# Both query halves of a head pair in one stage, for batches 0 and 1 as well

## The chip, the core and the metric

The kernel runs on one core of one Trainium2 chip. The metric is the device time of one execution in microseconds (us). The median of three runs of the kernel before is 2141.41 us (2141.41 to 2141.47). Everything is computed in fp32.

## What is computed

The inputs are x (16 batches of 1024 nodes with 256 channels), a sparse-valued 1024 x 1024 matrix adj that is stored dense, and small weights. There are two layers, each ended by a LayerNorm over the channels. Cut to what matters:

```python
# layer 0, for each batch; fea is x transposed (256 x 1024)
c_adj = mean(fea, axis=1)                      # one mean for each node
A  = |(|sigmoid(c_j - c_i) - 0.5|) - 0.5| * 2  # 1024 x 1024
g  = relu((fea @ (adj * sym(A))) * para)       # "query graph": q = g transposed
k, v = split(x @ kv_w)                         # 4 heads of 64 channels
out = softmax(q k^T * scale) v
x1  = layernorm(x + out)
# layer 1
h = relu(x1 @ w1_loop + adj @ (x1 @ w1_neigh) + b1)
h = relu(h  @ w2_loop + adj @ (h  @ w2_neigh) + b2)
y = layernorm(x1 + (x1 + h) * 0.5)
```

## The kernel before

**The order of work.** `run()` (L1029) writes the order of all instructions by hand: it stands under a manual schedule, so each engine works its own queue strictly in the order of the program text. The engines are TensorE (PE), VectorE (DVE), ScalarE (ACT), GpSimd (POOL), and SyncE (SP), which issues the DMAs. For each batch b there are five blocks of work: the attention of b, layer 1 (the graph convolution) of earlier batches, the query graph of b+1, the LayerNorm of b, and the keys and values of b+1.

**The attention** (class `Attention`, L623). The four heads form two head pairs, and the 1024 queries two halves of 512, so there are four units, numbered 2 * pair + half. `scores(u)` (L637) makes for each of eight key tiles two matmuls, one for each head of the pair; each uses 64 of the 128 rows of the array, so that two run side by side. ACT takes the exponential into an SBUF tile `pr`, and DVE adds the eight `pr` tiles up (`collect`, L665) and folds the sum into `den_part` (`partial`, L674). `outputs(u)` (L687) multiplies the `pr` tiles with v into one PSUM tile `av`, `turn(u)` (L700) transposes it on DVE into a tile `o`, and `add(units)` (L705) sums the denominators with one small matmul into `den_ps`, takes reciprocals, scales `o` and adds it to x (the tile `xB`). That last step is the "fold" of a unit. A batch can do a unit at a time (scores, outputs), or both halves of a pair: `both_scores(pair)` (L683) makes 16 score tiles in a row, and `two_units(pair)` (L1109) then makes both outputs. Before the change, batches 0 and 1 go a unit at a time, and batches 2 to 15 take both halves.

**PSUM** has eight banks of 512 fp32 values for each partition. The kernel cuts them into three "big" tiles of two banks (`big_psum`, `half_psum`, L85 to L89) and two "bank" tiles of one bank (`bank_psum`, L91). A score tile takes a big tile; but under `both_scores` every fourth one, from the third on, is *split* and takes the two bank tiles instead (L643 to L645). A tile can be taken again only when its last reader is through.

**SBUF rows.** Most working tiles (pr, adj, wg, o of even units, xB and so on) come from one pool of 31 row tiles (`row_tile`, L99).

**The query graph.** In batch 0 the class `Queries` (L483) builds the queries of batch 1: for each of eight row tiles t it loads a tile of adj, makes the likeness on ACT (two activations), multiplies by adj on DVE (`times_adj`, L513), and does four matmuls (`step`, L517), which accumulate into two big PSUM tiles `g_ps`; `end` (L526) reads them on DVE. Later batches use `FastQueries` (L533) with fewer multiplications.

**The LayerNorm of layer 0** (`BlockedNorm`, L319): `mean` and `squares`; `sum_squares` on DVE; `variance` (L343), which is a small matmul into `sum2`, one DVE instruction that writes `rstd`, and a power of -0.5 of a 128 x 32 tile on POOL (L347); `scale` (L349), two DVE multiplications by that result; and `spread` (L354), two DVE transposes and eight DMAs that store it.

**Keys and values of the next batch** (`KeysValues.run`, L428): seven products for each, in a Strassen-like form, with PSUM tiles `k_ps` (big) and `v_ps` (bank). It takes two callbacks, `between` after the fifth pair of products and `later` after the sixth. Four DVE additions stand behind `later` in the text, and the last two of them are the last readers of a big tile (`k_next`) and of a bank tile (`v_next`):

```python
            between()
            k_next, v_next = half_psum(f"k_ps_{b}_2"), bank_psum(f"v_ps_{b}_2")
...
            later()
            add(kT[:, 1, FB:N], u3, p7)
            add(block(1, 1), tiles(z3), tiles(y7))
...
            add(kT[:, 1, 0:FB], u1, k_next)
...
            add(block(1, 0), tiles(z1), tiles(v_next))
```

In batch 0 `later` holds `norm.scale()`, `norm.spread()` and four DVE transposes of adj tiles (`turn_adj((2, 3))`); `norm.variance()` is called earlier, ahead of `step(7)`. In batches 1 to 14 the order is `kv.run(norm.variance, q.scale)`, with `norm.scale` and `norm.spread` after `kv.run`.

**Layer 1** (`GraphConv`, L790): batch 1 does the first half of batch 0's convolution alone (`inner`, `first`); from batch 2 on `Joined` (L957) shares the products with adj between two batches. The last batch ends in `ending` (L910), which puts the bias b2 into PSUM by ACT (`bias`, L935) and lets the matmuls of `outer` (L870) accumulate onto it.

Of the kernel before, what the change touches and what calls it, by code (L numbers as in the profile page):

```python
# [10 lines left out]
F32 = mybir.dt.float32  # L11
# [7 lines left out]
def kernel(  # L19
# [603 lines left out]
    class Attention:  # L623
# [76 lines left out]
        def turn(self, u):  # L700
            name, pav = f"o_{self.b}_{u}", self.o[u]
            self.o[u] = work.tile([P, FB], F32, tag="o", name=name) if u % 2 else row_tile(name)[:, 0:FB]
            nc.vector.transpose(self.o[u], pav)
# [86 lines left out]
    class GraphConv:  # L790
# [68 lines left out]
        def second(self, quarters, between=None):  # L859

            self.uT = row_tile(f"uT_{self.b}")
            for j in range(NJ):
                pu = half_psum(f"u_ps_{self.b}_{j}")
                self.neighbours(j, pu, range(TJ), quarters)
                if j and between:
                    between()
                self.neighbours(j, pu, range(TJ, NT), quarters)
                nc.scalar.copy(self.uT[:, ts(j, FB)], pu)

        def outer(self, g, per, p2, onto=False):  # L870
            for i in range(per):
                t = g * per + i
                nc.tensor.matmul(p2[:, ts(i, C)], self.uT[:, ts(t, P)], w2n_sb, start=not onto, stop=False,
                                 skip_group_check=onto)
                nc.tensor.matmul(p2[:, ts(i, C)], self.h1T[:, ts(t, P)], w2l_sb, start=False, stop=True,  # L875
                                 skip_group_check=onto)
# [8 lines left out]
        def last(self):  # L885
            per = N // C
            for g in range(NT // per):
                p2 = big_psum(f"h2_ps_{self.b}_{g}")
                self.outer(g, per, p2)
                self.residual(g, per, p2)  # L890

# [18 lines left out]
        def ending(self, dst, quarters, aside):  # L910
# [24 lines left out]
            def bias(g):  # L935
                banks[g] = (bank_psum if g % 2 else half_psum)(f"h2e_ps_{g}")
# [14 lines left out]
            self.second(quarters, lambda: (bias(0), bias(1), aside(), bias(2), bias(3), quarter(0)))  # L951
# [77 lines left out]
    def run():  # L1029
# [57 lines left out]
        for b in range(B):  # L1087
# [30 lines left out]
            if more and not c1:  # L1118
                for u in range(len(UNITS)):
                    att.scores(u)  # L1120
                    if u:
                        att.add(u - 1)
                    att.outputs(u)
                    if u == 2:
                        for t in range(3):
                            q.load(t)
                            q.weigh(t)
                    if u == 0:
                        NodeSums(q, xb, str(b + 1)).all()
            elif more and not both:  # L1130
                att.scores(0)
                att.outputs(0)
                NodeSums(q, xb, str(b + 1)).all()
                kv = KeysValues(b + 1, channel_major(blocked, f"xT_{b + 1}"))
                att.scores(1)
                kv.sums()
                att.add(0)
                att.outputs(1)
                for t in (0, TJ):
                    q.load(t)  # L1140
                c1.inner()
                q.left(nc.gpsimd)
                for t in (0, TJ):
                    q.likeness(t)
                for ij, n in QUARTERS.items():
                    store(n, quarters[ij])
                c1.first(quarters, lambda: (att.add(1), adj_sums(quarters, 1), adj_sums(quarters, 2), weigh_first()))
                c1.turn_blocks()
                att.scores(2)
                att.outputs(2)  # L1150
                for t in (1, TJ + 1):
                    q.load(t)
                    q.likeness(t)
                    q.times_adj(t)
                att.scores(3)
                for t in (2, TJ + 2, 3, TJ + 3):
                    q.load(t)
                for t in (2, TJ + 2, 3, TJ + 3):
                    q.likeness(t)
                q.right(1)  # L1160
                att.add(2)
                att.outputs(3)
            elif more:
# [6 lines left out]
                both.fetch("00", "10")  # L1170
                c2.load_x()
# [7 lines left out]
                both.fetch(2, 3)  # L1179
                nodes.line()  # L1180
                both.fetch(1)
                nodes.row()
                for t in (0, TJ):
                    q.load(t)
                both.fetch(4, "11")
                c1.inner()
                both.left(nc.gpsimd)
                both.run({1: (lambda: q.left(nc.gpsimd),),
                          2: (lambda: att.add(0, 1),),
                          6: (lambda: q.likeness(0), lambda: c3 and c3.moments()),  # L1190
                          7: (lambda: q.likeness(TJ),),
                          5: (weigh_first,),
                          4: (lambda: c3 and c3.finish(out[b - 3]),)})
                c2.last()
# [20 lines left out]
            if more and not c1:  # L1215
# [8 lines left out]
                q.times_adj(4)  # L1224
                q.step(1)
                att.add(3)
# [4 lines left out]
                q.times_adj(5)  # L1231
                q.step(2)
                q.step(3)
                norm.mean()
                q.times_adj(6)
                q.times_adj(7)
                q.step(4)
                norm.squares()
                norm.sum_squares()
                q.step(5)  # L1240
# [3 lines left out]
                norm.variance()  # L1244
                xB = load_blocked(b + 1, f"a{b + 1}")
                q.step(7)
                qT = q.end()
                load_next()
                kT, v = kv.run(later=lambda: (norm.scale(), norm.spread(), turn_adj((2, 3))))
                turn_adj((5, 6, 7))  # L1250
            elif more:
                q.pair(2)
                q.step(0)
                q.step(1, lambda: att.add(*((2, 3) if both else (3,))), 5)
# [37 lines left out]
        c2.last()  # L1292
        c1.turn(1)
        c2.moments()
        c1.ending(out[B - 1], quarters, lambda: c2.finish_aside(out[B - 2]))
# [70 lines left out]
```

## Time and profile before

| What | Value |
|---|---|
| Median of the runs | 2141.41 us |
| The profiled execution: time, span of its instructions | 2141.32 us, 2139.5 us (1.8 us lie around the span) |
| Busy: PE, DVE, ACT, POOL | 2127.3, 1889.8, 1046.4, 342.9 us |
| Mean granted TensorE clock | 0.998 of full speed |
| Batch 0, attention (first score matmul to first `g_ps` matmul) | 49.70 to 107.05 us |
| Batch 0, query graph, and keys and values | 107.05 to 135.29, 135.29 to 147.73 us |
| Batch 1, attention with the convolution of batch 0 | 147.73 to 225.90 us |
| Batch 1, query graph, and keys and values | 225.90 to 250.49, 250.49 to 263.15 us |
| Batch 2 begins | 263.15 us |
| Last matmul of the convolution begins | 2128.33 us |

"Busy" of PE counts every matmul from its start to its modelled end, so 99% does not say that the array runs at its peak: a stage in which PE waits a little between matmuls shows up as a longer stage. It is read from the start times of one stage and the next. In the timeline a line is a run of equal instructions: start, time from the first to the last end, engine, source line, operation, output and inputs, shapes, count; the brackets give the idle time of the engine ahead of it and what ended it. A 512-column fp32 matmul is recorded as two instructions.

### The profile page before, as it was taken

The numbers are of one execution on the slowest core, as the hardware profiler recorded it, in microseconds if no ns is written. First come the engines' busy times: TensorE is split into PE (matmuls) and PEld (weight loads), VectorE is DVE, ScalarE is ACT, GpSimd is POOL, SyncE is SP. The second block draws the span as 40 slices with busy tenths as digits, with TensorE's granted clock in tenths as the row PEclk, the third lists the DMA queues.
The fourth block names the chain that finished last, engine by engine and source line by source line (L and its number), as shares of the span: only waits on it lengthen the run. The fifth ranks groups of instructions, "written<-read, shape, count | busy, mean of one in ns | idle before, by whom it ended". The sixth has DMA issues, their size and how long they took to land.

```text
span 2139.5 us, 24050 instructions
## 1 busy us (share of the span) xinstructions
PE 2127.3 (99%) x8356; PEld 1028.0 (48%) x8356; DVE 1889.8 (88%) x2360; ACT 1046.4 (49%) x1486; POOL 342.9 (16%) x187
## 2 busy tenths in 40 slices
PE   9999999999999999999999999999999999999998
PEld 5344444544445455454554444544445444544454
DVE  5999998989899898988989899899898999989964
ACT  5745545545355452555625555355553445545412
POOL 1011120121302113030130301303012130121021
PEclk9999999999999999999999999999999999999999
DMA  9495675737677365763747638466473665734544
GB/s 236 128 141 185 133 224 139 180 123 124 208 165 208 95 123 212 158 217 97 140 177 156 217 118 152 154 148 216 131 173 130 138 217 146 180 118 96 163 157 157
DMA packets 611393, 341.09 MB, mean 159 GB/s; under 512 B 491712, under 2 KB 556608, under 8 KB 611264
## 3 DMA queue, kind: packets, MB, share of 16 engines
q1 hardware_dynamic: 610992, 339.21, 60.5%
q8 instruction: 68, 1.11, 0.2%
q14 instruction: 61, 0.50, 0.1%
q10 hardware_dynamic: 272, 0.26, 0.0%
HBM read 289.54 MB, written 49.87 MB: 159 GB/s over the span
## 4 chain that ended last, share of the span: by engine, by line


## 5 line engine op out<-in xcount | busy, mean ns | idle before, releaser
L672 DVE TENSOR_TENSOR acc<-acc,pr 128x1024 f32<-128x1024 f32 x384 | 473.2, 1232 | 37.1 <-ACT pr L656 0.7
L658 ACT ACTIVATE pr<-s 128x1024 f32<-128x1024 f32 x400 | 397.4, 1116 | 143.7 <-PE s L651 143.7
L651 PE MATMUL s<-qT,kT 64*128 64x512 f32 x2048 | 450.3, 593 | 0.0
L693 PE MATMUL av<-pr,v 128*64 128x512 f32 x2048 | 447.4, 594 | 0.0
L651 PEld LDWEIGHTS s<-qT,kT 64*128 64x128 f32 x2048 | 196.1, 187 | 236.4 <-issue 182.2
L693 PEld LDWEIGHTS av<-pr,v 128*64 128x64 f32 x2048 | 143.8, 137 | 295.6 <-issue 271.6
L347 POOL TENSOR_TENSOR rstd<-rstd,neg_half 128x32 f32<-128x32 f32 x16 | 99.8, 6236 | 1118.7 <-DVE rstd L345 1118.7
L988 PE MATMUL hu_ps<-adj,R 128*128 128x512 f32 x480 | 211.8, 594 | 0.0
L509 ACT ACTIVATE wg<-c_row,c_sums 128x1024 f32<-128x1024 f32 x120 | 137.0, 1142 | 85.6 <-DVE den_part L680 65.8
L515 DVE SCALAR_TENSOR_TENSOR wg<-wg,adj 128x1024 f32<-128x1024 f32 x128 | 150.1, 1210 | 11.8 <-ACT wg L510 11.8
L988 PEld LDWEIGHTS hu_ps<-adj,R 128*128 128x128 f32 x480 | 90.1, 190 | 108.1 <-issue 105.0
L510 ACT ACTIVATE wg<-wg 128x1024 f32<-128x1024 f32 x128 | 135.3, 1057 | 4.1
L656 ACT ACTIVATE pr<-s 128x512 f32<-128x512 f32 x224 | 133.8, 710 | 0.3 <-PE s L651 0.3
L596 PE MATMUL g_ps<-T,S 128*128 128x512 f32 x224 | 116.6, 602 | 0.2 <-DVE T L570 0.2
L596 PE MATMUL g_ps<-wg,S 128*128 128x512 f32 x224 | 115.6, 597 | 0.0
L596 PE MATMUL g_ps<-wg,x 128*128 128x512 f32 x224 | 109.0, 599 | 0.0
L808 ACT COPY t<-t_ps 128x1024 f32<-128x1024 f32 x16 | 16.2, 1014 | 189.6 <-PE t_ps L805 189.6
L988 PE MATMUL hu_ps<-adj,t 128*128 128x512 f32 x240 | 105.7, 592 | 0.0
L605 ACT COPY P<-g_ps 128x512 f32<-128x512 f32 x14 | 8.2, 586 | 183.9 <-DMA xB<-in_x_dram 103.1
L880 DVE TENSOR_TENSOR z<-h_ps,b_sb 128x1024 f32<-128x1024 f32 x30 | 36.7, 1224 | 59.4 <-PE h_ps L875 59.4
L979 POOL TENSOR_TENSOR R<-h 128x512 f32<-128x512 f32 x14 | 28.1, 2009 | 358.2 <-DMA adj<-adjT 261.6
L677 DVE STREAM_TRANSPOSE accB<-acc 128x1024 f32<-128x1024 f32 x64 | 79.7, 1245 | 2.2
(204 smaller groups left out, 3115.7 us busy)
## 6 DMA issues: line engine op xcount, KB each, us to landing
adj<-adjT SPq DMA_DIRECT2D x210, 512.0 KB
adj<-in_adj_dram SPq DMA_DIRECT2D x128, 512.0 KB
para<-in_L_gnn_para_dram SPq DMA_DIRECT2D x32, 512.0 KB
xB_a<-in_x_dram SPq DMA_DIRECT2D x128, 128.0 KB
x1d<-xB_a SPq DMA_DIRECT2D x128, 128.0 KB
x<-x1d SPq DMA_DIRECT2D x16, 1024.0 KB
xB<-in_x_dram SPq DMA_DIRECT2D x120, 128.0 KB
x<-in_x_dram SPq DMA_DIRECT2D x15, 1024.0 KB
```

The costliest lines, as they stand in the source:

```text
L347: nc.gpsimd.tensor_tensor(self.rstd, self.rstd, neg_half, ALU.pow)
L509: nc.scalar.activation(wg, self.c_row, AF.Abs, bias=self.c_col[:, t:t + 1], scale=-1.0)
L510: nc.scalar.activation(wg, wg, AF.Tanh, scale=-0.5 / C)
L515: nc.vector.scalar_tensor_tensor(wg, wg, 1.0, self.adj.pop(t), op0=ALU.add, op1=ALU.mult)
L596: nc.tensor.matmul(self.p[n], x_n[:, k, :], w_n, start=(k == 0), stop=(k == TJ - 1))
L651: nc.tensor.matmul(halves[s], self.kT[rows, pair, ts(mt, P)], self.qT[rows, pair, ts(j, FB)], start=True, stop=True)
L656: nc.scalar.activation(pr[:, ts(s, FB)], halves[s], AF.Exp)
L658: nc.scalar.activation(pr, ps, AF.Exp)
L672: nc.vector.tensor_add(self.acc, self.acc, prs[mt])
L677: nc.vector.transpose(accB, self.acc)
L693: nc.tensor.matmul(pav[s * HD:(s + 1) * HD, :], self.v[:, mt, pair * P + s * HD:pair * P + (s + 1) * HD], prs[mt][:, ts(s, FB)], start=(mt ...
L988: nc.tensor.matmul(dst, self.x[n][:, k, :], of_rows(rows, k), start=(start and k == 0), stop=(k == TJ - 1), skip_group_check=again)
```

## The change

The edits, in the order of the program:

1. **Batch 0** makes `both_scores(0)`, the node sums of the next batch, `two_units(0)`, `both_scores(1)`, the first three loads and weighings of the query graph, `two_units(1)`. Before, it made scores and outputs of one unit after the other, and folded a unit in the next one's scores.
2. **The folds of batch 0** move into the query graph: `add(0, 1)` ahead of `step(1)` and `add(2, 3)` ahead of `step(2)`. The weighings (`times_adj`) of later tiles and `norm.mean`, `norm.squares` shift by a step or two.
3. **The LayerNorm of batch 0**: `sum_squares` now comes after the query graph's end, and `norm.variance` is the `between` of `kv.run`. `later` is unchanged and stands behind it.
4. **Batch 1** takes the path of the batches from 2 on (`both_scores`, `two_units`), without what belongs to `Joined`; the fold of units 0 and 1 is one call in the convolution, the fold of units 2 and 3 one call in the query graph.
5. **turn**: unit 1 of batch 0 gets its `o` from the row tiles instead of the one `o` tile.
6. **outer**: only the first matmul into each bank carries the flag that starts an accumulation; before, each 256-column block carried one.
7. **ending**: the four banks that receive the bias are now banks that matmuls have just filled (the two of `second`, and the last tile of the convolution before), not fresh ones; the fourth bias is written after `second`.

```diff
-            self.o[u] = work.tile([P, FB], F32, tag="o", name=name) if u % 2 else row_tile(name)[:, 0:FB]
+            late = u == len(UNITS) - 1 or u % 2 and self.b
+            self.o[u] = work.tile([P, FB], F32, tag="o", name=name) if late else row_tile(name)[:, 0:FB]
...
-                nc.tensor.matmul(p2[:, ts(i, C)], self.uT[:, ts(t, P)], w2n_sb, start=not onto, stop=False,
-                                 skip_group_check=onto)
+                first = not onto and i % (FB // C) == 0
+                nc.tensor.matmul(p2[:, ts(i, C)], self.uT[:, ts(t, P)], w2n_sb, start=first, stop=False,
+                                 skip_group_check=not first)
...
-                banks[g] = (bank_psum if g % 2 else half_psum)(f"h2e_ps_{g}")
+                banks[g] = (self.pu[0], filled[:, 0:FB], filled[:, FB:N], self.pu[1])[g]
...
-            self.second(quarters, lambda: (bias(0), bias(1), aside(), bias(2), bias(3), quarter(0)))
+            self.second(quarters, lambda: (bias(0), bias(1), bias(2), aside(), quarter(0)))
+            bias(3)
...
             if more and not c1:
-                for u in range(len(UNITS)):
-                    att.scores(u)
-                    if u:
-                        att.add(u - 1)
-                    att.outputs(u)
...
+                att.both_scores(0)
                 NodeSums(q, xb, str(b + 1)).all()
+                two_units(0)
+                att.both_scores(1)
+                for t in range(3):
                     q.load(t)
+                    q.weigh(t)
+                two_units(1)
             elif more:
                 att.both_scores(0, summed=False)
...
+                else:
+                    q.left(nc.gpsimd)
+                    for t in (0, TJ):
+                        q.likeness(t)
+                    for ij, n in QUARTERS.items():
+                        store(n, quarters[ij])
+                    c1.first(quarters, lambda: (att.add(0, 1), adj_sums(quarters, 1), adj_sums(quarters, 2),
+                                                weigh_first()))
...
                 q.times_adj(3)
                 q.step(0)
                 q.times_adj(4)
+                att.add(0, 1)
                 q.step(1)
-                att.add(3)
+                q.times_adj(5)
+                att.add(2, 3)
                 att.watch()
...
                 q.step(4)
+                q.step(5)
+                norm.mean()
                 norm.squares()
-                norm.sum_squares()
-                q.step(5)
                 q.step(6)
                 kv.sums()
                 kv.load()
-                norm.variance()
                 xB = load_blocked(b + 1, f"a{b + 1}")
                 q.step(7)
                 qT = q.end()
+                norm.sum_squares()
                 load_next()
-                kT, v = kv.run(later=lambda: (norm.scale(), norm.spread(), turn_adj((2, 3))))
+                kT, v = kv.run(norm.variance, lambda: (norm.scale(), norm.spread(), turn_adj((2, 3))))
                 turn_adj((5, 6, 7))
             elif more:
...
-                q.step(1, lambda: att.add(*((2, 3) if both else (3,))), 5)
+                q.step(1, lambda: att.add(2, 3), 5)
```

## The prediction

> **What bounds the kernel.** I read the page's busy times first, then the timeline of PE from the first batch to the third, then those of DVE and POOL around the seams between the batches, and last the end of the run.
>
> ```profile
> span 2139.5 us, 24050 instructions
> ...
> PE 2127.3 (99%) x8356; PEld 1028.0 (48%) x8356; DVE 1889.8 (88%) x2360; ACT 1046.4 (49%) x1486; POOL 342.9 (16%) x187
> ```
>
> PE is busy for 99% of the span and DVE for 88%, so time is won or lost only where PE's stages get shorter or where another engine makes PE wait. PE's timeline, of batch 0's first units, the seam from batch 1 to 2, and a first stage of batch 2 with both halves:
>
> ```profile
> 49.70 7.14 PE L651 MATMUL s<-qT,kT 64*128 64x512 f32 x32
> 56.76 7.09 PE L693 MATMUL av<-pr,v 128*64 128x512 f32 x32
> 63.78 7.14 PE L651 MATMUL s<-qT,kT 64*128 64x512 f32 x32
> 70.85 0.41 PE L712 MATMUL den_ps<-den_part,fold 128*128 128x32 f32 x2
> 71.19 7.09 PE L693 MATMUL av<-pr,v 128*64 128x512 f32 x32
> 78.20 7.14 PE L651 MATMUL s<-qT,kT 64*128 64x512 f32 x32
> ...
> 257.57 0.31 PE L257 MATMUL sum_ps<-sq_part,fold 128*128 128x32 f32 x2
> ...
> 263.15 14.00 PE L651 MATMUL s<-qT,kT 64*128 64x512 f32 x64
> 277.08 13.95 PE L693 MATMUL av<-pr,v 128*64 128x512 f32 x64
> 290.96 3.84 PE L805 MATMUL t_ps<-w1n_sb,x1T 128*128 128x128 f32 x32
> ```
>
> The columns are start, duration, line, tiles, count. Stages follow each other without a gap in both forms. A pair costs 78.20 - 49.70 = 28.50 us unit by unit, 0.34 of it a denominator matmul between two stages, and 290.96 - 263.15 = 27.81 with both halves. So the prize is 0.35 for each switch from scores to outputs and back that is saved, plus the denominator: under 1 us a pair, four pairs.
>
> DVE's timeline at the seam from batch 0 to 1, and POOL's:
>
> ```profile
> 131.98 0.19 DVE L345 TENSOR_SCALAR rstd<-sum_ps 128x32 f32<-128x32 f32 x1 [0.27 <-PE sum_ps L257]
> ...
> 139.67 2.35 DVE L352 TENSOR_TENSOR xB_a<-xB_a,rstd 128x1024 f32<-128x1024 f32 x2
> 141.94 2.36 DVE L227 STREAM_TRANSPOSE x1T<-xB_a 128x1024 f32<-128x1024 f32 x2
> 144.23 2.45 DVE L1071 STREAM_TRANSPOSE adjT<-adjB 128x512 f32<-128x512 f32 x4
> ...
> 148.36 0.68 DVE L480 TENSOR_TENSOR v<-vsnap,v_ps 128x512 f32<-128x512 f32 x1
> ```
>
> ```profile
> 132.25 5.46 POOL L347 TENSOR_TENSOR rstd<-rstd,neg_half 128x32 f32<-128x32 f32 x1 [83.79 <-DVE rstd L345]
> ```
>
> Here POOL's 5.46 us power ends at 137.71, before DVE wants it at 139.67: hidden. DVE then needs 9.37 us (139.67 to 148.36 + 0.68) from the first multiplication to the addition that frees the last `v_ps` bank.
>
> **Part by part.** Batch 0, attention: 57.35 us now (49.70 to 107.05). Two pairs of 27.81 are 55.62: -1.73. Its folds move into the query graph: two denominators of 0.16 (one of that size stands in batch 2, 303.23 to 303.39) for one of 0.14, +0.18. The `sum2` matmul moves into the keys and values; that stage takes 12.44 in batch 0 (135.29 to 147.73) and 12.66 with it in batch 1 (250.49 to 263.15), while the query graph loses 0.15: +0.07. Sum -1.48.
>
> Does DVE keep up there? The first addition comes 3.15 us after the scores (2000.60 and 2003.75 in batch 15, which has this very order), a pair's additions and folds take 23.25 (333.00 to 356.25). Pair 1 starts at 49.70 + 27.81 = 77.51, so DVE is through at 103.91, its first weighing (1.15) at 105.1; `step(0)` can start at 105.32. Then 3.45 a step on PE against 1.15 a weighing and 4.95 for each fold (a reciprocal pair 0.72, six operations of 0.7): weighing 5 ends near 117, step 5 starts near 122.9. Hidden, by 0.2 us at the head. One doubt: the `av` tile of unit 2 is read only after three weighings, near 108.0, and the graph's two PSUM tiles need two of three big ones. If they get that one, PE waits 1.0 or 2.7; if not, 0. I take 0, as the last scores leave two free, and keep 2.7.
>
> Batch 1: 78.17 us from 147.73 to 225.90 becomes two times 27.81 plus the convolution's 21.16 between them, 76.8: -1.37. The query graph in the form of the later batches takes 24.81 (357.15 to 381.96) for 24.59: +0.22. Sum -1.15. DVE's folds shrink by four reciprocals.
>
> **The seam is where it turns.** In `kv.run` the new `between` issues `sum2`, and `later` still begins with `norm.scale`, which needs POOL's result. DVE is in order; behind that multiplication it holds the transposes, the four adj transposes and the four additions. Let S be the start of batch 1's scores. `sum2` starts at S - 5.58 (257.57 against 263.15), DVE's `rstd` 0.35 later (257.92), POOL 0.27 later, for 5.46 us: ready at S + 0.50. Plus 9.37: the `v_ps` bank is free at S + 9.87. Who waits for it? The third score tile is now split and needs both bank tiles. Before, batch 1 used big tiles only, so this addition was nobody's business. What such a wait looks like stands in batch 15, second pair:
>
> ```profile
> 2000.60 15.06 PE L651 MATMUL s<-qT,kT 64*128 64x512 f32 x64
> 2015.59 13.95 PE L693 MATMUL av<-pr,v 128*64 128x512 f32 x64
> ```
>
> ```profile
> 2002.02 1.30 DVE L703 STREAM_TRANSPOSE o<-av 128x512 f32<-128x512 f32 x2
> ...
> 2003.38 0.30 PEld L651 LDWEIGHTS s<-qT,kT 64*128 64x128 f32 x4 [0.77 <-DVE o L703]
> ```
>
> The bank came free at 2003.32, the weights load at 2003.38, and the stage is 14.99 long instead of 13.93. The third tile would start at S + 2 x 0.87 = S + 1.74; at the new seam it starts at S + 9.93. PE stands still for **8.2 us**; all of PE's queue is behind it, so all of it reaches the end. Bounds: POOL's power is 5.44 with DVE quiet (2053.31) and 6.36 beside DVE's multiplications (258.19); DVE is quiet here, so I take 5.46 and keep 9.1 as the upper end. Lower: 8.2 less 2.4 if the adj transposes are not in the way, less 0.9 if one half of the split tile gets through early.
>
> The rest time has a price of its own that no row shows in mid-run. The end shows what the clock does when PE rests (columns: stretch, sum, busy us of PE, PEld, DVE, ACT, POOL, then granted clock):
>
> ```profile
> 2130.00:2132.00 2.00, 0.00 (x0) 0.00 (x0) 1.76 (x6) 1.00 (x2) 0.89 (x2) 0.97 0.40 131
> 2132.00:2134.00 2.00, 0.00 (x0) 0.00 (x0) 0.82 (x3) 0.09 (x1) 0.70 (x1) 0.50 0.43 145
> ```
>
> The last matmul starts at 2128.85, and about 3 us later the granted clock is 0.50. The new rest is over twice that. What the return costs I bound from the start of the run: PE's first 16 transposes took 3.47 us (1.48 to 4.95), the next 16 2.21 (4.95 to 7.16), so 1.26 lost; at 0.50 through 3.47 us it would be 1.74; or nothing. I take 1.3, the measured row. The Trainium skill ("TensorE: Matmul & The Clock Gate", Part 1, the clock gate) says that an idle window of about 3.4 us halves the clock and that some 4 us of work bring it back. By that rule, which speaks against this change, the return would cost about 2 us, and the time would be 0.7 higher, an estimate from that page.
>
> After the wait DVE is no worse off than usual: its additions start at S + 9.87 + 3.6 (six adj transposes), 5.3 us after PE's shifted start; in batch 2 it is 8.05 (271.20 - 263.15) without a stall.
>
> The other edits: `turn` takes a row tile, the same instruction. `outer` changes a flag. The ending writes the same four biases of 0.55; the fourth follows `second` on ACT and would be ready near 2124.9, its matmul starts at 2127.03, so 2.1 us of cover; `aside` starts 0.5 later, and ends near 2121.4, 2.4 before ACT's next copy at 2123.78. I cost all of it at 0; without the cover it is 0.55 at most.
>
> **Sum.** -1.48 - 1.15 + 8.2 + 1.3 = +6.9. The profiled execution took 2141.32 (span 2139.5 and 1.8 around it), so its own sum is 2148.2; the median of the runs, 2141.41, lies 0.1 higher: **2148.3**.
>
> **Rivals.**
> - *The seam stays covered* (not slower): the power is ready, or the split tile finds two free banks, by S + 1.74. For it: in batch 2 the same addition runs at 263.25 and nobody waits. Against: there `q.scale`, not `norm.scale`, stands in `later`, and POOL is awaited afterwards; to decide, the power would have to end 8.2 us earlier. Then only the savings are left: 2141.4 - 2.6 = 2138.8.
> - *More waits*: `g_ps` gets the tile of unit 2 (2.7), or DVE's backlog reaches batch 1's second pair. With the upper ends of the seam, 9.1 and 1.7: 2152.3.
> - *The change does not do what it says*: both halves in one stage save nothing here, since ACT's exponentials set the pace. Against: the 27.81 of batch 2 is with 16 exponentials. It gives 2141.4 + 9.5 = 2150.9.
>
> **Numbers.** The forecast has 0.74, the covered seam 0.18, more waits 0.05, no saving 0.03. The forecast's own bounds are 2147.0 (no clock price) to 2152.3 (all upper ends); the two lower bounds of the wait bring it to 2143.7. That range holds 0.80; the covered seam is left out. No change, within 0.2% (4.3 us, about what a measurement of this kernel can tell from none), is the covered seam without its tail plus a sliver of the forecast: 0.17. Faster by more than that needs savings that I do not see: 0.03. Slower: 0.80.
>
> **What would show it.** Each pair of batches 0 and 1 takes 27.8 us on PE, batch 1's first apart; that one's scores take some 22 to 24, with one gap after the second tile, and the load that ends it names DVE's L480 of the new file. DVE stands idle for some 5 us ahead of `norm.scale`, released by POOL. The granted clock dips below 1 near 150 us. I am wrong if that gap is under 2 us, if the first `g_ps` matmul of batch 0 comes much later than 105.3, or if much more than 11.2 us (2139.5 - 2128.33) lie between the last convolution matmul and the end of the span.

## The result, and the profile after

The changed kernel takes **2152.56 us** (median of six runs, 2151.27 to 2153.16); the kernel before took 2141.52 in the same comparison. The ratio is 1.0048, with a 95% interval of 1.0038 to 1.0058: slower by half a per cent. The predicted time was 2148.3, and the upper end of its range, 2152.3, lies 0.3 below the measured median. The profiled execution is the longest of the six, 2153.16, which is 11.84 above the profiled one of before. The page:

```profile
span 2151.4 us, 24038 instructions
...
PE 2128.8 (99%) x8348; PEld 1029.3 (48%) x8348; DVE 1890.2 (88%) x2352; ACT 1047.5 (49%) x1502; POOL 346.7 (16%) x187
```

The busy times hardly differ from before (most on POOL, by 3.8 us, which is busy for 16%). So the 12 us are waits, and the page's shares can't show where. PE's timeline does (start, duration, line, tiles, count, and in brackets PE's idle time and what ended it):

```profile
50.90 14.00 PE L651 MATMUL s<-qT,kT 64*128 64x512 f32 x64
64.83 13.95 PE L693 MATMUL av<-pr,v 128*64 128x512 f32 x64
78.72 14.00 PE L651 MATMUL s<-qT,kT 64*128 64x512 f32 x64
...
147.43 2.84 PE L651 MATMUL s<-qT,kT 64*128 64x512 f32 x10
157.41 14.70 PE L651 MATMUL s<-qT,kT 64*128 64x512 f32 x54 [7.14 <-DVE v L480]
172.05 13.95 PE L693 MATMUL av<-pr,v 128*64 128x512 f32 x64
...
207.09 14.00 PE L651 MATMUL s<-qT,kT 64*128 64x512 f32 x64
222.74 13.95 PE L693 MATMUL av<-pr,v 128*64 128x512 f32 x64 [1.65 <-ACT pr L658]
```

In batch 0 a pair takes 78.72 - 50.90 = 27.82, as forecast. In batch 1 the first scores stop after ten records (two whole tiles and the first half of the split one), PE stands for 7.14 us until DVE's L480 frees the bank, and the stage is 172.05 - 147.43 = 24.62 long instead of 13.93. In the second pair there is another wait, for ACT's probabilities, which the forecast did not have. Here is DVE at the seam:

```profile
142.21 0.19 DVE L345 TENSOR_SCALAR rstd<-sum_ps 128x32 f32<-128x32 f32 x1 [2.33 <-PE sum_ps L257]
147.97 2.36 DVE L352 TENSOR_TENSOR xB_a<-xB_a,rstd 128x1024 f32<-128x1024 f32 x2 [5.57 <-POOL rstd L347]
...
156.68 0.68 DVE L480 TENSOR_TENSOR v<-vsnap,v_ps 128x512 f32<-128x512 f32 x1
...
160.87 1.19 DVE L670 TENSOR_TENSOR acc<-pr,pr 128x1024 f32<-128x1024 f32 x1
```

DVE stands for 5.57 us ahead of `norm.scale`, released by POOL's power, and everything behind it is late: the first sum of probabilities starts 13.44 us after batch 1's first score matmul (160.87 - 147.43). Before it was 4.83 (152.56 - 147.73). This is the row of before:

```profile
152.56 1.18 DVE L670 TENSOR_TENSOR acc<-pr,pr 128x1024 f32<-128x1024 f32 x1
```

That number returns below. The clock (columns: stretch, its length, busy us of PE, PEld, DVE, ACT, POOL, granted clock, DMA share, GB/s):

```profile
152.00:153.00 1.00, 0.00 (x0) 0.00 (x0) 1.00 (x2) 0.00 (x0) 0.00 (x0) 0.54 1.15 141
162.00:163.00 1.00, 1.00 (x8) 0.43 (x6) 0.90 (x2) 0.54 (x2) 0.00 (x0) 0.84 0.00 0
```

The first stretch is 0.54 on average, so the clock fell to a half at 152.1, 1.8 us after the last matmul; the second is 0.84, so it came back at 162.3, 4.9 us after PE resumed.

The account of the two profiled executions, each term from start times of stages:

| Where | Forecast | Measured |
|---|---|---|
| Up to batch 0's first scores | 0 | +1.20 |
| Batch 0: attention; graph, keys and values | -1.73; +0.25 | -1.71; +0.21 |
| Batch 1 without its waits | -1.15 | -1.39 |
| Seam: PE's rest at the split tile | +8.2 | +8.24 |
| Seam: slow clock behind it | +1.3 | +2.45 |
| Second pair of batch 1: wait for probabilities | 0 | +1.72 |
| Query graph of batch 2 | 0 | +0.37 |
| Ending | 0 | +0.69 |

The sum is 11.78 for 11.84. Two small terms are not in the table and nearly cancel: the last convolution takes 0.32 more, since the one-column matmul into `good_ps`, which stood behind the last matmul before, now runs inside it (at 2085.81); and from DVE's last instruction to the end of the span it is 0.24 less. (The rest of 8.24 is 157.41 less 149.17, where a score stage that doesn't wait would begin its third tile; the trace's 7.14 is shorter since half of that tile ran.)

### The profile page after: what moved, and what is told of

Its sections match the earlier page's. It is cut to its first block, busy times and chain, and to the rows that moved or that the text cites. A ratio compares the mean times of both kernels' runs of the same rounds, so it can differ in the third digit from the quotient of the medians.

```text
span 2151.4 us, 24038 instructions
## 1 busy us (share of the span) xinstructions
PE 2128.8 (99%) x8348; PEld 1029.3 (48%) x8348; DVE 1890.2 (88%) x2352; ACT 1047.5 (49%) x1502; POOL 346.7 (16%) x187
## 4 chain that ended last, share of the span: by engine, by line
## 5 line engine op out<-in xcount | busy, mean ns | idle before, releaser
L658 ACT ACTIVATE pr<-s 128x1024 f32<-128x1024 f32 x384 | 385.9, 1125 | 140.0 <-PE s L651 137.5
L347 POOL TENSOR_TENSOR rstd<-rstd,neg_half 128x32 f32<-128x32 f32 x16 | 99.8, 6237 | 1119.6 <-DVE rstd L345 1119.6
L656 ACT ACTIVATE pr<-s 128x512 f32<-128x512 f32 x256 | 152.6, 707 | 8.8 <-PE s L651 8.8
```

Of the source, the lines that this page charges most:

```text
L347: nc.gpsimd.tensor_tensor(self.rstd, self.rstd, neg_half, ALU.pow)
L656: nc.scalar.activation(pr[:, ts(s, FB)], halves[s], AF.Exp)
L658: nc.scalar.activation(pr, ps, AF.Exp)
```

## The experiments

**The theory** to be tested is that of the forecast: POOL's power, no longer hidden, makes DVE late, the bank of `v_ps` comes free late, and PE's rest at the split tile and the slow clock behind it are the price, 10.7 us. **The main rival**, from the second wait: DVE is the bound all through batch 1, and PE's rest at the seam only shows it first, so that what is won at one place is lost at the next. One table holds what the traces show of batch 1, in all kernels but ending_only (below), which leaves batch 1 as it was. "DVE" is from the first score matmul to DVE's first sum; "to batch 2" ends with the first score matmul there.

| Kernel | Median | DVE | First scores | Second scores, outputs | To batch 2 |
|---|---|---|---|---|---|
| before | 2141.41 to 2141.79 | 4.83 | by units | by units | 115.42 |
| changed | 2152.56 | 13.44 | 24.62 | 15.65, 13.89 | 126.44 |
| seam_later | 2149.02 | 11.20 | 13.93 | 20.54, 16.16 | 122.92 |
| seam_variance | 2145.80 | 4.83 | 13.94 | 16.22, 13.88 | 116.33 |
| warm_rest | 2165.92 | 13.43 | 37.96 | 15.65, 13.89 | 139.78 |
| no_split | 2151.77 | 13.44 | 23.64 | 15.65, 13.89 | 125.46 |
| warm_eight | 2152.39 | 13.43 | 22.18 | 16.56, 15.45 | 126.49 |
| batch1_only | 2143.91 | 4.83 | 13.94 | 16.20, 15.58 | 118.00 |
| no_power | 2146.90 | 7.90 | 16.65 | 16.55, 15.50 | 120.98 |
| adj_back | 2142.51 | 4.98 | 13.93 | 16.35, 15.58 | 118.16 |
| others_mended | 2149.49 | 13.43 | 25.00 | 13.93, 13.88 | 125.11 |
| both_mended | 2139.35 | 4.98 | 13.94 | 13.94, 13.88 | 114.04 |

**seam_later: the additions ahead of `norm.scale`.**

```diff
-                kT, v = kv.run(norm.variance, lambda: (norm.scale(), norm.spread(), turn_adj((2, 3))))
-                turn_adj((5, 6, 7))
+                kT, v = kv.run(norm.variance)
+                norm.scale()
+                norm.spread()
+                turn_adj((2, 3, 5, 6, 7))
```

> The changed kernel, but in batch 0 the multiplication by the deviation (norm.scale), the transposes and all adj transposes stand behind the four additions of kv.run, so that no v_ps bank waits for POOL's power. Theory (the stall at the third score tile is that wait, with the slow clock behind it): the first scores of batch 1 take 13.9 to 14.2 us instead of 24.62, and the time is 10.7 lower than the changed kernel's, about 2141.8. Rival (PE waits at the seam for something else, DVE's backlog or the tiles of the form with both halves itself): the scores stay above 20 us and the time above 2149. Half of each would show as 2145 to 2147.

The first scores take 13.93 us: the rest at the split tile is gone, and it was the wait for `v_ps`. But the time is 2149.02 (ratio to before 1.0033, 1.0020 to 1.0046), 3.5 below the changed kernel and not 10.7. Neither expectation held whole: the scores are those of the theory, the time is that of the rival. PE in the second pair:

```profile
217.13 16.23 PE L693 MATMUL av<-pr,v 128*64 128x512 f32 x64 [6.54 <-ACT pr L658]
```

PE comes to the second pair 10.7 us earlier against the start of the batch, but DVE's sums start only 2.2 us earlier (11.20 against 13.44). Of the 10.69 won, 7.16 are lost again here. ACT's own row in the changed kernel says what it is waiting for:

```profile
221.67 1.94 ACT L658 ACTIVATE pr<-s 128x1024 f32<-128x1024 f32 x2 [2.10 <-DVE accB L677]
```

The exponentials stop after twelve of sixteen tiles, until DVE's transpose of the sum of unit 2 (`accB`) has read the sum `acc`. With both halves in one stage 16 `pr` tiles are wanted at once, and the pool of 31 row tiles has no free one until DVE is through with that sum. (That it is a row is read from the releaser and the code; a larger pool was not tried.) So in batch 1 PE waits for DVE by way of ACT and of a row tile.

**seam_variance: the variance hidden again, `norm.scale` left ahead of the additions.**

```diff
                 q.step(6)
+                norm.sum_squares()
                 kv.sums()
                 kv.load()
+                norm.variance()
...
-                norm.sum_squares()
...
-                kT, v = kv.run(norm.variance, lambda: (norm.scale(), norm.spread(), turn_adj((2, 3))))
+                kT, v = kv.run(later=lambda: (norm.scale(), norm.spread(), turn_adj((2, 3))))
```

> The changed kernel with the sum of squares and the variance back ahead of the last steps of batch 0's query graph, as the kernel before has them; norm.scale stays ahead of the four additions. So the order on DVE in kv.run is that of the changed kernel, and only POOL's power is earlier. Theory (the price is POOL's 5.46 us standing open ahead of norm.scale, not the place of norm.scale): no stall at the seam, about 2141.8. Rival (norm.scale, the transposes and the adj transposes ahead of the additions are too long by themselves, 9.4 us): the first scores of batch 1 take 17 us or more, and the time is 2145 or above.

First scores 13.94: with the power hidden, the order on DVE alone costs nothing, as the theory has it. DVE's sums are back at 4.83, and batch 1 is 10.1 us shorter than in the changed kernel. The time, 2145.80 (1.0021; 1.0011 to 1.0030), is still 4 above the theory's, for two reasons that the trace shows. The `sum2` matmul now stands too early on PE, ahead of DVE's sum of squares, and PE rests there for 1.78 us, with 1.70 of slow clock behind it (a step that takes 3.68 took 5.38). And the second pair's wait is 2.29, for 1.72 in the changed kernel.

**warm_rest and warm_eight: extra matmuls in PE's rest.** They repeat the first half of the split tile ahead of the wait for its second half; `range(28)` in the first, `range(8)` in the second:

```diff
+                if (b, u, mt) == (1, 0, 2):
+                    for _ in range(28):
+                        nc.tensor.matmul(halves[0], self.kT[0:HD, pair, ts(mt, P)], self.qT[0:HD, pair, ts(j, FB)],
+                                         start=True, stop=True)
```

> The changed kernel with 28 extra matmuls of 0.22 us (6.1 us together) on the first half of the split score tile, ahead of the wait for its second half: work that writes what the tile gets anyway, and fills the 7.14 us for which PE rests. DVE and POOL, and so the end of the wait, stay as they are. Theory (2.45 us of the 10.69 at the seam are the slow clock after the rest): the granted clock stays near 1.0, the 14 tiles behind the wait take 12.2 us instead of 14.64, and the time is 2.2 to 2.5 lower, about 2150.1. Rival (the tiles behind the wait are slow for another reason, ACT's exponentials or DVE's backlog): they stay at 14.6 and the time within 0.5 of the changed kernel's.

> The changed kernel with 8 extra matmuls on the first half of the split tile, in place of the 28 of the run before. That run showed that one such matmul by itself takes 0.84 us, so that 28 took 23.5 us and overran the rest; 8 take 6.7 of the 7.14 us. Theory (the clock takes 2.2 to 2.5 us behind the rest): the granted clock stays at 1.00, the tiles behind the wait take 12.5 us as there instead of 14.64, and the time is about 2.2 lower than the changed kernel's, 2150.3. Rival (what is won there is lost again, since DVE is behind all through batch 1 and lets PE wait later): the first scores are 2.2 shorter and the second pair's wait of 1.72 grows by most of that, so that the time stays within 0.5 of the changed kernel's.

In warm_rest the extra work was mis-sized: a 64-row matmul by itself takes 0.84 us, since the 0.44 of the stages is that of two heads side by side. The 28 overran the rest by some 16 us. What it still shows: the clock stayed at 1.00, and the tiles behind it took 12.5 us. warm_eight, of the right size:

```profile
148.27 7.03 PE L651 MATMUL s<-qT,kT 64*128 64x512 f32 x16
...
156.42 12.28 PE L655 MATMUL s<-qT,kT 64*128 64x512 f32 x54 [0.27 <-DVE v L480]
...
220.24 15.53 PE L697 MATMUL av<-pr,v 128*64 128x512 f32 x64 [2.56 <-ACT pr L662]
```

The tiles behind the wait take 12.21 (168.63 - 156.42) instead of 14.64, so the 2.4 us were the clock's. And yet the median is 2152.39, as in the changed kernel: of the 2.44 won in the first scores, 0.91 come back as a longer wait in the second pair and 1.56 in its outputs, at a slow clock that this longer wait brought on. From start to start batch 1 is as long as in the changed kernel, 126.49 against 126.44. This is the rival's case: the slow clock at the seam was real, and free.

**no_split: big tiles only in the first pair of batch 1.**

```diff
-                split = first is not None and (first + mt) % 4 == 2
+                split = first is not None and (first + mt) % 4 == 2 and (b, pair) != (1, 0)
```

> The changed kernel, but the first pair of batch 1 takes no split score tiles: all sixteen are big ones, as in the kernel before. The order on DVE is unchanged, so the last v_ps bank comes free as late as in the changed kernel. Theory (PE waits for the bank tile, and with big ones alone it waits for the slot of k_ps that the addition of the keys frees, or for no one): if the third tile takes the slot of the first one, the stall is below 1 us and the time about 2142 to 2143; if it takes that of the last k_ps, whose addition stands just ahead of the last v_ps one, the stall is 7 to 8 us and the time stays near 2152. Rival (the backlog of the sums on DVE sets the pace of batch 1's first pair, whatever the tiles): the two scores and outputs of that pair together stay above 38 us, with PE waiting for probabilities or for av.

```profile
156.07 14.32 PE L651 MATMUL s<-qT,kT 64*128 64x512 f32 x56 [7.40 <-DVE kT L478]
```

The second case of the theory: the third tile takes the slot of the last `k_ps`, whose addition (L478) stands one instruction ahead of L480. The split form is not at fault: in either form the third tile waits for those additions. 2151.77 (1.0046; 1.0029 to 1.0062).

**batch1_only: batch 0 and the tail behind it as before.** (The blocks of batch 0 in `run()` are those of the kernel before; the rest is the changed kernel.)

```diff
             if more and not c1:
-                att.both_scores(0)
-                NodeSums(q, xb, str(b + 1)).all()
-                two_units(0)
...
+                for u in range(len(UNITS)):
+                    att.scores(u)
+                    if u:
+                        att.add(u - 1)
+                    att.outputs(u)
...
-                kT, v = kv.run(norm.variance, lambda: (norm.scale(), norm.spread(), turn_adj((2, 3))))
+                kT, v = kv.run(later=lambda: (norm.scale(), norm.spread(), turn_adj((2, 3))))
```

> The changed kernel with batch 0 and the tail behind it (folds, mean, variance) as in the kernel before: only batch 1 takes both halves in one stage, and the ending is the changed one. The power on POOL is hidden again, and DVE enters batch 1 as early as in the kernel before. Theory (the wait of the second pair's scores in batch 1 comes from DVE's lateness, which POOL's power and the folds of batch 0 bring about): no stall at the seam, second scores of batch 1 at most 0.5 us over 13.93, so 2141.5 - 1.15 + 0.7 for the ending, about 2141. Rival (both halves in one stage need more row tiles than there are, whatever DVE does): that wait stays at 1.7 us or more, and the time is 2142.8 or above.

```profile
213.80 15.65 PE L693 MATMUL av<-pr,v 128*64 128x512 f32 x64 [2.20 <-ACT pr L658]
```

The rival's side: DVE is as early as in the kernel before (4.83), there is no rest at the seam, and PE still waits 2.20 us in the second pair, with 1.70 of slow clock behind it. 2143.91 (1.0011; 1.0002 to 1.0021). So the second wait does not need batch 0. Both halves in one stage want the rows earlier than DVE's work ahead of that pair allows.

**no_power: the price of POOL's power itself.** (The power of batch 0 is left out, so that its result is the variance.)

```diff
-            nc.gpsimd.tensor_tensor(self.rstd, self.rstd, neg_half, ALU.pow)
+            if self.name != "0":
+                nc.gpsimd.tensor_tensor(self.rstd, self.rstd, neg_half, ALU.pow)
```

> The changed kernel without POOL's power behind the variance of batch 0 (its result is then the variance in place of the deviation's inverse; nothing else is left out). The 5.5 us for which DVE stands still ahead of norm.scale go, and everything behind it on DVE comes 5.5 us earlier against the start of batch 1's scores. Theory A (what counts is PE's own rest at the split tile): the rest shrinks from 8.2 to 2.7 us, too short for the slow clock, the second pair's scores stay at 15.65, and batch 1 gets shorter by 5.5 + 2.45: 118.5 us from its first scores to those of batch 2, 2144.6 in all. Theory B (from the seam on DVE is the bound, and PE only waits for it at one place or at another): batch 1 gets shorter by DVE's 5.5 us and no more, or less with a slow clock at the other place: 120.5 to 122, the second pair's scores at 17 to 18.5, 2146.5 to 2148.2 in all.

```profile
151.18 12.28 PE L652 MATMUL s<-qT,kT 64*128 64x512 f32 x54 [1.59 <-DVE v L481]
...
214.98 15.57 PE L694 MATMUL av<-pr,v 128*64 128x512 f32 x64 [2.54 <-ACT pr L659]
```

(The source lines behind L347 are one higher here.) The first scores are 7.97 shorter, 5.5 for the rest and 2.45 for the clock, as theory A has it; the second pair is 2.51 longer, as theory B has it; batch 1 is shorter by 5.46, DVE's own 5.54 (7.90 against 13.44). 2146.90 (1.0025; 1.0015 to 1.0034). Theory B holds in batch 1's length and in the time, as long as DVE's work behind the seam stands in this order. Its second scores, 17 to 18.5, did not come: they took 16.55, and the rest of the loss is in the outputs, at a slow clock (15.50 for 13.89).

**ending_only: the edits of the ending alone, on the kernel before** (items 6 and 7 of the change).

```diff
...
-                banks[g] = (bank_psum if g % 2 else half_psum)(f"h2e_ps_{g}")
+                banks[g] = (self.pu[0], filled[:, 0:FB], filled[:, FB:N], self.pu[1])[g]
...
```

> The kernel before with the edits of the ending alone: biases in the banks of u_ps and of the last joined tile, the flag in outer. Theory (the third quarter's matmuls wait for DVE's read of the second quarter, since both are halves of one two-bank tile): 0.7 us above the kernel before, all of it behind the last u_ps matmul, with a wait of 0.9 us for DVE's x ahead of one h_ps matmul. Rival (the 0.7 seen in the changed kernel is a difference from run to run): the stretch from the last u_ps matmul to the end is as in the kernel before within 0.1, and so is the time within 0.3.

The median is 2142.95 against 2141.79; the interval, 0.9996 to 1.0015, takes in no change, so the time alone settles nothing. The traces do. From the start of the last adj matmuls into `u_ps` (L856, L857 in the changed kernel) to that of DVE's last instructions (L308) it is 12.76 us in the kernel before and 13.45 here, and 13.45 or 13.46 in the changed kernel, seam_later, seam_variance and no_power, which have this ending too. (Of the 1.16 between the medians the wait is 0.7; the trace shows another 0.32 where the matmul into `good_ps` now runs.) PE in the changed kernel:

```profile
2136.32 0.60 PE L877 MATMUL h_ps<-w2l_sb,h1T 128*128 128x256 f32 x2
2137.86 0.67 PE L875 MATMUL h_ps<-w2n_sb,uT 128*128 128x256 f32 x2 [0.94 <-DVE x L947]
```

The third quarter's matmuls wait until DVE has read the second quarter's result. The two are different banks, but halves of one tile (`filled`).

**both_mended, adj_back, others_mended: three mends, together and in part.** The first has them all:

```diff
-                banks[g] = (self.pu[0], filled[:, 0:FB], filled[:, FB:N], self.pu[1])[g]
+                banks[g] = (self.pu[0], filled[:, 0:FB], self.pu[1], filled[:, FB:N])[g]
...
-            self.second(quarters, lambda: (bias(0), bias(1), bias(2), aside(), quarter(0)))
-            bias(3)
+            self.second(quarters, lambda: (bias(0), bias(1), bias(3), aside(), quarter(0)))
+            bias(2)
...
-                    c1.first(quarters, lambda: (att.add(0, 1), adj_sums(quarters, 1), adj_sums(quarters, 2),
-                                                weigh_first()))
+                    c1.first(quarters, lambda: (att.add(0, 1), adj_sums(quarters, 1), weigh_first()))
...
-                q.step(2)
                 q.times_adj(6)
+                q.step(2)
                 q.step(3)
-                q.times_adj(7)
                 q.step(4)
-                q.step(5)
                 norm.mean()
+                q.times_adj(7)
+                q.step(5)
                 norm.squares()
+                norm.sum_squares()
                 q.step(6)
+                norm.variance()
...
-                norm.sum_squares()
...
-                kT, v = kv.run(norm.variance, lambda: (norm.scale(), norm.spread(), turn_adj((2, 3))))
+                kT, v = kv.run(later=lambda: (norm.scale(), norm.spread(), turn_adj((2, 3))))
...
-                kT, v = kv.run(norm.variance, q.scale)
+                if c2:
+                    kT, v = kv.run(norm.variance, q.scale)
+                else:
+                    kT, v = kv.run(lambda: (adj_sums(quarters, 2), norm.variance()), q.scale)
```

adj_back undoes the third and the last of these hunks (the adj sums); others_mended undoes the seam's, the fourth to the sixth.

> The changed kernel with three edits. The mean of batch 0 directly after the folds, its squares and variance ahead of the last step of the query graph, so that POOL's power is hidden. The adj sums of the third block in batch 1 moved from ahead of the second pair (2.7 us of DVE) into the keys and values, where DVE waits for 2 us. In the ending the halves of the shared tile two quarters apart. Theory (all that the change loses is DVE's lateness at these three places): no stall at the seam, second scores of batch 1 at most 0.3 us over 13.93, no wait in the ending, and the savings of 2.6 us are left: 2138.9. Rival (DVE is full from the end of batch 0 on, and the savings on PE turn into waits further on): 2140.5 or above, with PE waiting for DVE or for probabilities in batch 1 or 2.

> The mended kernel (2139.35) with one of its three edits undone: the adj sums of the third block stand ahead of the second pair of batch 1 again, 2.7 us of DVE. Theory (the tile of the twelfth probabilities waits for DVE's sums of the unit before, and 2.7 us of DVE decide on it): PE waits 2.0 to 2.5 us in the second pair's scores, with up to 1.7 more behind it at a slow clock, as in the kernel with batch 1 alone: 2141.4 to 2143.5. Rival (the mended order of the tail of batch 0 covers it): below 0.5 us of wait, and 2139.3 to 2139.8.

> The changed kernel with the two later edits of the mended one, the adj sums of the third block moved and the halves of the shared tile two quarters apart; the seam between batches 0 and 1 is that of the changed kernel. Against the mended kernel it prices the seam alone. Theory (the seam costs PE's rest and the clock, 10.7 us, once DVE has room behind it): 2150.0, with first scores of 24.6 us and second scores of at most 14.2. Rival (DVE's lateness from the seam comes to light at the second pair all the same): second scores above 15 us, and 2151.2 or more.

both_mended takes **2139.35 us** (eleven runs, 2139.14 to 2140.01), ratio 0.9989 to before, 0.9980 to 0.9998: 2.4 us faster than the kernel before, and 13.2 faster than the changed one. PE in batch 1, from the mended kernel:

```profile
146.57 14.00 PE L651 MATMUL s<-qT,kT 64*128 64x512 f32 x64
160.51 13.95 PE L693 MATMUL av<-pr,v 128*64 128x512 f32 x64
...
195.55 14.00 PE L651 MATMUL s<-qT,kT 64*128 64x512 f32 x64
209.49 13.96 PE L693 MATMUL av<-pr,v 128*64 128x512 f32 x64
```

No bracket is left. Batch 0, from its first scores to those of batch 1, takes 96.53 (146.57 - 50.04) for 98.03 before, batch 1 114.04 for 115.42: the savings of 1.50 and 1.38 are there. The ending is back at 12.76.

```profile
211.84 15.65 PE L693 MATMUL av<-pr,v 128*64 128x512 f32 x64 [2.35 <-ACT pr L658]
```

That row is adj_back's. It takes 2142.51 (1.0003; 0.9993 to 1.0013), no longer clear of the kernel before: 2.7 us of DVE work ahead of the second pair cost 4.12 us of batch 1 (118.16 against 114.04), because the wait of 2.35 brings the clock down as well. others_mended is 2149.49 (1.0037; 1.0024 to 1.0049), with first scores of 25.00 and no second wait: against both_mended its batch 1 is 11.07 longer, all of it in the first scores. So where DVE has room behind the seam, the whole price of rest and clock is paid.

## Why the prediction was right, and where it was not

**What held.** The direction, and the mechanism in its order: `sum2` behind the fifth pair of products, POOL's power standing open, 5.57 us of DVE idle (forecast some 5), the bank free 9.93 us after the first score (forecast 9.87), a rest of 8.24 (forecast 8.2) that ends with L480 of DVE. Of the signs, two did not come as named: batch 1's first scores took 24.62, for 22 to 24, and its second pair 29.54, for 27.8. seam_variance and no_power show POOL's part, seam_later the additions' part. The time came out 4.3 us above the forecast; the four terms below and in the table that it had too small or at 0 (the clock, the second pair, the ending, batch 2's query graph) make 3.9 of that. The savings were right to 0.02 us in batch 0. Batch 1 saved 1.39 for 1.15. There the forecast added 0.22 for the form of the query graph, which took 24.58 against 24.59; without it, its own lines give just 1.39 (78.17 - 2 x 27.81 - 21.16). The doubt about `g_ps` was rightly left at 0: the graph of batch 0 began without a wait.

**The step that was mis-sized: the clock's return, 1.3 us, measured 2.45.** The forecast took it from the first matmuls of the run. But the granted clock reads 1.00 there from the start (0 to 7 us, both kernels), so that row does not show a clock that returns. What sets the price is how long the clock stays at a half after PE resumes, 4.9 us here, half of which is lost. It is no constant: after the long rests of no_split, seam_later and others_mended it was 3.8, 4.6 and 5.7. The rule of the Trainium skill that the forecast weighed ("TensorE: Matmul & The Clock Gate", Part 1, the clock gate), some 4 us of work until the clock is back, gave about 2, and was the nearer of the two.

**The step that was wrong: the ending at no cost, measured +0.69.** The cover of each bias was looked at, and held. What was not looked at is which tiles the banks now belong to: two quarters in a row share a tile, and the matmuls of the one wait for the reads of the other. others_mended and both_mended, with the halves two quarters apart, show the same 12.76 as the kernel before. The sign that the forecast named for an error here looked in the wrong place: from the last convolution matmul to the end it is 10.4 us, less than the 11.2 of before, since the wait lies ahead of that matmul.

**The step that stopped too early: "after the wait DVE is no worse off than usual".** For the first pair this holds: counted as the forecast does, from PE's shifted start, the sums come after 5.2 us (forecast 5.3). But it was not followed to the second pair, where the probabilities need rows that DVE frees. That is +1.72, a case that the rival *more waits* named with a small chance, and without a price. Its own reason, a backlog from the seam, is not needed: batch1_only has the wait without one. It is 2.7 us of DVE work in the convolution that decides (adj_back).

**What the sum hid.** The forecast added the clock's price to the rest as if PE alone set the end. It gave the size of the loss at the seam nearly right, but not what bounds it: in the changed kernel PE's rest and DVE's lateness limit batch 1 one after the other, and 7.16 of 10.69 us, or all of 2.44, taken off the first came back at the second.

**Left open.** The 1.20 us ahead of batch 0's first scores are a wait for a DMA of x in code that is not changed; in the profiles of the other kernels those scores begin between 49.70 and 50.59, so I take it for a difference between executions, which is not shown. The 0.37 of batch 2's query graph comes, in the changed kernel, with one wait of 0.22 for DVE's `T`. The kernel before has a wait like it in a later batch (at 1560.41). In batch 2 it is there in seven of the kernels with both halves in batch 1 and absent in four (batch1_only, seam_variance, adj_back, others_mended), and I have no cause that fits all of them.

## What to carry to other kernels

A small result that another engine computes should be asked for well before the engine that needs it gets there: what stands behind the waiting instruction in its queue is late by the whole latency, and so is each tile that it would have freed. When a stage is made shorter on the busiest engine, add up what the second busiest has to do until the next tile it must free: a gap that is closed at one place can open at the next (7.16 of 10.69 us here), and then only a mend of both shows the gain. In this kernel two banks of one tile kept their waits in common (0.94 us), so halves that are in use at the same time should come from different tiles.

## What the hardware showed that I had not expected

**The half clock comes in steps of 3.4 us, and a rest of under 2 us can bring it on.** Read in stretches of 0.5 us (one with a clock between 1 and 0.5 holds the turn, at that share), the granted clock stood at 0.50 for 3.41 us after rests of 1.78 (seam_variance, in batch 0), 2.20 (batch1_only), 2.35 (adj_back), 2.54 (no_power) and 2.56 (warm_eight); for 6.83 after those of 6.54 (seam_later) and 7.40 (no_split), and for 10.24 after those of 7.14 and 7.13 (the changed kernel, others_mended). It did not fall at all after rests of 1.59 (no_power), 1.65 (the changed kernel, warm_rest, no_split) and 2.22 (seam_variance, second pair). Here is the one of adj_back, where PE had rested from 209.49 to 211.84, and was at work again for a microsecond before the clock fell:

```profile
211.00:213.00 2.00, 1.16 (x6) 0.48 (x8) 2.00 (x2) 2.00 (x3) 0.00 (x0) 0.99 0.00 0
213.00:216.00 3.00, 3.00 (x10) 0.78 (x8) 2.69 (x4) 1.60 (x3) 0.00 (x0) 0.50 0.00 0
216.00:217.00 1.00, 1.00 (x6) 0.34 (x4) 1.00 (x1) 0.00 (x0) 0.00 (x0) 0.81 0.00 0
```

So a wait of 2.3 us costs 2.3 in one place and 4.0 in another.

**What decides is where the rest falls.** The falls of the clock lie on a grid that runs through the whole execution. In the changed kernel the clock fell at 152.09 and, behind the last matmul, at 2145.47: 1993.38 us apart, 584 times 3.4133 (a third of 10.24). In the other eight kernels in which it fell in mid-run, these two falls lie 563 to 587 times that length apart, each within 0.02 us of a whole number. Now lay the rests on that grid. The 2.20 us of batch1_only lie within one step of 3.41, and the clock fell at its end; the 2.22 of seam_variance are cut into 1.60 and 0.62 by the border of two steps, and it did not fall. In the step that ended with a fall, PE always rested for 1.78 us or more; 1.65 or less never brought one. The border between is not sharp: one step at the end of seam_later, with 1.92 of rest, brought none. After the long rests the clock came back at the end of the first step that PE had filled.

The Trainium skill, in the same part of "TensorE: Matmul & The Clock Gate", says that activity is judged in windows of about 3.4 us that run freely; the grid agrees. Its rule of thumb, no idle gaps of more than some 3.4 us, is too mild by the measured rests of 1.78 to 2.56, and the measurement decides. The kernels with a rest near the border also scatter more (adj_back from 2140.85 to 2144.06; both_mended, without such a rest, from 2139.14 to 2140.01). That this is the grid falling differently from run to run fits, but only one run of each has a trace, so it is not shown.
